# Queries of a second self attention by seven block products instead of eight, with the sums spread over the step order

## The chip, the cores and the metric

The kernel runs on one core of a Trainium2 chip. The metric is the device time of one launch in microseconds. The kernel is called several times; the median of the runs counts.

## The reference

A two-layer decoder over `x` of shape (8, 112, 512) in float32, six residual steps: layer 0 self attention, cross attention and a ternary feed forward, then layer 1 self attention, cross attention and a mixture feed forward. The change is in the layer 1 self attention (and, in name only, in the same function for layer 0). Cut to what matters (b = 8, s = 112):

```python
B, S, D = x.shape          # D = 512, H = 16 heads of DH = 128, 4 key heads
q = (x @ Wq.T).reshape(b, s, 16, 128)
k = (x @ Wk.T).reshape(b, s, 4, 128)
v = (x @ Wv.T).reshape(b, s, 4, 128)
q = q * cos + rotate_half(q) * sin          # the same for k
k, v = repeat(k, 4), repeat(v, 4)           # four query heads share a key head
scores = einsum('bhqd,bhkd->bhqk', q, k) * 128 ** -0.5
attn = softmax(scores)                      # the window masks nothing at s = 112
out = einsum('bhqk,bhkd->bhqd', attn, v).reshape(b, s, 2048)
return out @ Wo.T
```

## The kernel before

The 8 x 112 tokens are kept transposed in two halves `xT[hf]` of four batches (448 columns, four chunks of 128 features). `self_attention` (L526 on) runs eight turns (g, hf): four groups g of four query heads, each for both token halves. `pipeline` writes out TensorE's order by hand: while the scores and contexts of turn n are done, `weave` puts the steps of `prepare(n + 1)` and the output projections between them as filler, by a cost given with each step. The order on VectorE, ScalarE, GpSimd and SyncE is made by the scheduler of the tile framework, from the program's order and its own estimates.

One turn's preparation is one key tile `pr_k` and four query tiles `pr_q`. In `roped` (L605) a tile is four accumulating matmuls over 448 columns into one bank (`mm`, two buffers). ScalarE copies the bank to `raw` (L614), two DMAs of SyncE's queue write the rotated halves to `turned`, GpSimd multiplies `raw` with the cosines (L623), VectorE `turned` with the sines (L624), and GpSimd adds both (L625).

A turn has two units of two batches. `scores` (L677) fills a two-bank tile (`s`, two buffers). `softmax` takes the maximum on VectorE (L450), eight exponentials with sums on ScalarE (L453), the reciprocal on VectorE (L456), and multiplies on GpSimd (L460). TensorE transposes (L471), VectorE copies (L472), and `contexts` multiplies with the values (L695) into two `mm` banks that ScalarE copies to `oT` (L700).

The output projection of two neighbouring token tiles is already done by seven products: `out_pair` (L714 on) forms sums of blocks of `oT` (`os`, `block_sums`, L249 to L252) and differences of blocks of `Wo` (`wos`, one `lay(g)` of four instructions, L257 to L260, as one step at the end of a turn), and `sevens` (L262 on) runs the products 1, 6, 2 and 5, 7, 3, 4 over 256 columns. A set holds two banks at a time: 1 and 2 share bank x, 6 stands alone in y, then 5 and 3 share a new y, 7 and 4 a new z. After each product `put` reads the bank (ScalarE L747 for the first, VectorE L744 for the rest), and the next product in the same bank waits for that read. The tiles that make no pair go through `project_out` (L426, L430, read at L431).

Of the kernel before, what the change touches and what calls it, by code (L numbers as in the profile page):

```python
# [9 lines left out]
F32 = mybir.dt.float32  # L10
# [5 lines left out]
P = 128  # L16
# [141 lines left out]
def decoder(ctx: ExitStack, tc: tile.TileContext, i: dict, out: bass.AP):  # L158
# [84 lines left out]
        for k, (lhsT, rhs) in enumerate(pairs):  # L243
            nc.tensor.matmul(ps, lhsT, rhs, start=(k == 0), stop=(k == len(pairs) - 1))  # L244

    def block_sums(engines, s, a11, a12, a21, a22):

        e1, e2 = engines
        e1.tensor_tensor(s[0], a21, a22, ALU.add)  # L249
        e2.tensor_tensor(s[2], a11, a21, ALU.subtract)  # L250
        e1.tensor_tensor(s[1], s[0], a11, ALU.subtract)
        e1.tensor_tensor(s[3], a12, s[1], ALU.subtract)  # L252

    def block_differences(engines, t, b11, b12, b21, b22):

        e1, e2 = engines
        e1.tensor_tensor(t[0], b12, b11, ALU.subtract)  # L257
        e2.tensor_tensor(t[2], b22, b12, ALU.subtract)
        e1.tensor_tensor(t[1], b22, t[0], ALU.subtract)
        e1.tensor_tensor(t[3], b21, t[1], ALU.subtract)  # L260

    def sevens(products, put, width, name):  # L262


        bank = {}

        def product(n, at):
            pairs = products(n)
            for k, (lhsT, rhs) in enumerate(pairs):
                nc.tensor.matmul(  # L270
                    bank[at], lhsT, rhs, start=(k == 0 and n in (1, 6, 5, 7)), stop=(k == len(pairs) - 1),
                    skip_group_check=True,
                )
            put(n, bank[at])

        def first():
            for at in "yx":
                bank[at] = mm(f"p{at}_{name}")[:, :width]
            product(1, "x")
            product(6, "y")  # L280
            product(2, "x")

        def second():
            for at in "yz":
                bank[at] = mm(f"p{at}2_{name}")[:, :width]
            product(5, "y")
            product(7, "z")
            product(3, "y")
            product(4, "z")

        return first, second
# [234 lines left out]
    def self_attention(layer, following=None, behind=None, xT=None):  # L526
# [4 lines left out]
        half = width // 2  # L531
        turns = [(g, hf) for g in range(G) for hf in range(2)]
        held, matrices = [{} for _ in turns], {}
        dq, wos = [], {}

        if l0:
            pool, mid, top, tpool = (
# [50 lines left out]
        def extra(n):  # L588
            if n < 1:

                first, last = (0, 3 if l0 else 2) if n < 0 else (6, 8)
                steps = [(3.4, lambda b=b: values(b)) for b in range(first, last)]
                return steps + ([] if l0 or n < 0 else [(0.0, lambda: lay(0))])
            if not l0:
                return [] if n % 2 or n == len(turns) - 2 else [(0.0, lambda: lay(n // 2))]
            if n == 6:
                return [(0.6, rope) for _, rope in joined[0]["ropes"][4:]]
            steps = [(0.0, lambda k=k: add_bias(k)) for k in range(NT)] if n == 1 else []
            if n < 5:
                steps += [(0.0, lambda k=k: ternary_sum(tpool, k)) for k in range(4 * n - 4, 4 * n)]  # L600
            elif n == 5:
                steps += [(0.1, ternary_mean), (0.0, begin)]
            return steps

        def roped(dst, w, at, xh, bias, which, name):  # L605

            cos, sin = (
                const(f"{n}{which}{layer}").unsqueeze(1).to_broadcast([P, HB, T]) for n in ("cos", "sin")
            )
            ps = mm(f"pr_{name}")  # L610
            accumulate(ps[:, :HT], [(w[:, c, at : at + P], xh[:, c, :]) for c in range(NC)])
            raw = top.tile([P, HT], F32, tag="raw", bufs=3, name=f"raw_{name}")
            if bias is None:
                nc.scalar.copy(raw, ps[:, :HT])  # L614
            else:
                nc.scalar.activation(raw, ps[:, :HT], AF.Identity, bias=bias)

            turned = top.tile([P, HT], F32, tag="turned", bufs=3, name=f"turned_{name}")
            for at in range(0, P, half):
                other = at ^ half  # L620
                issued.append(nc.sync.dma_start(out=turned[at : at + half, :], in_=raw[other : other + half, :]).ins)
            by_batch = lambda t: t.rearrange("p (b t) -> p b t", b=HB)
            nc.gpsimd.tensor_tensor(by_batch(dst), by_batch(raw), cos, ALU.mult)  # L623
            nc.vector.tensor_tensor(by_batch(turned), by_batch(turned), sin, ALU.mult)  # L624
            nc.gpsimd.tensor_tensor(dst, dst, turned, ALU.add)  # L625

        def prepare(n):
            g, hf = turns[n]
# [17 lines left out]
                if not l0:  # L646
                    steps += entering(npool, xT, "at1", [6], 3)
            steps += [(3.0, lambda: roped(kT, wk, g * P, xT[hf], col("bk", g) if l0 else None, "k", f"k_{nm}"))]
            for c in range(4):
                steps.append((3.0, lambda c=c: roped(  # L650
                    qT[:, c, :], wq, c * P, xT[hf], col("bq", 4 * g + c) if l0 else None, "q",
                    f"q_{nm}_{c}",
                )))
            if n == 1:
                steps += [(3.4, lambda b=b: values(b)) for b in (4, 5)]
            if l0 and n == 0:
# [28 lines left out]
        def contexts(n, u):  # L685
            g, hf = turns[n]
            nm = f"{layer}_{g}_{hf}_{u}"
            kept = {}

            def add():  # L690

                po = [wide(f"po_{nm}_0")[:, 0, :]] if l0 else [mm(f"po_{nm}_{k}") for k in range(2)]
                for k, (b, s) in enumerate(parts(n, u)):
                    at, kv = slice(s * width, (s + 1) * width), g * (P // width) + s
                    nc.tensor.matmul(  # L695
                        po[0 if l0 else k][at, :HT], v[:, b, kv * width : (kv + 1) * width],
                        kept["pT"][:, 4 * k : 4 * k + 4, :].rearrange("p h q -> p (h q)"), start=True, stop=True,
                    )
                for k, b in enumerate(sorted({b for b, _ in parts(n, u)})):
                    nc.scalar.copy(oT[:, :, rows_of(b)], po[k][:, :HT].rearrange("p (h q) -> p h q", h=4))  # L700

            return probs_transposed(late, lambda: held[n]["p", u], kept, nm) + [(0.8 if l0 else 1.5, add, True)]

        def lay(g):

            b = matrices[g][1].rearrange("p (h k) (s n) -> p h k s n", h=2, s=2)
            t = dq[0].tile([P, 4, 2, D // 2], F32, tag="wos", bufs=1, name=f"wos_{layer}_{g}")
            wos[g] = t
            block_differences(
                (nc.vector, nc.gpsimd), [t[:, n] for n in range(4)],  # L710
                b[:, 0, :, 0], b[:, 0, :, 1], b[:, 1, :, 0], b[:, 1, :, 1],
            )

        def out_pair(g, k, nm):  # L714
# [5 lines left out]
                return slice((k + m) * P, (k + m + 1) * P)  # L720

            def add_up():
                s.append(dq[0].tile([P, 4, 2, P], F32, tag="os", bufs=1, name=f"os_{nm}"))
                block_sums(
                    (nc.vector, nc.gpsimd), [s[0][:, n] for n in range(4)],
                    a[:, 0, :, tok(0)], a[:, 1, :, tok(0)], a[:, 0, :, tok(1)], a[:, 1, :, tok(1)],
                )

            def products(n):
                b = matrices[g][1].rearrange("p (h k) (s n) -> p h k s n", h=2, s=2)  # L730
                t, v = wos[g], s[0]
                pick = {
                    1: lambda c: (a[:, 0, c, tok(0)], b[:, 0, c, 0]), 2: lambda c: (a[:, 1, c, tok(0)], b[:, 1, c, 0]),
                    3: lambda c: (v[:, 3, c], b[:, 1, c, 1]), 4: lambda c: (a[:, 1, c, tok(1)], t[:, 3, c]),
                    5: lambda c: (v[:, 0, c], t[:, 0, c]), 6: lambda c: (v[:, 1, c], t[:, 1, c]),
                    7: lambda c: (v[:, 2, c], t[:, 2, c]),
                }
                return [pick[n](c) for c in range(2)]

            def put(n, ps):  # L740
                if n == 1:
                    d.append(dq[0].tile([P, 2, 2, D // 2], F32, tag="od", bufs=1, name=f"od_{nm}"))
                d1, d2, d3 = d[0][:, 0, 1], d[0][:, 1, 0], d[0][:, 1, 1]
                add = lambda to, of: nc.vector.tensor_tensor(to, of, ps, ALU.add)  # L744
                x0, x1 = x[:, k, : D // 2], x[:, k, D // 2 :]
                if n == 1:
                    nc.scalar.copy(d1, ps)  # L747
                elif n == 6:
                    add(d2, d1)
                elif n == 2:  # L750
# [8 lines left out]
                else:  # L759
                    add(d2, d2)  # L760
                    nc.gpsimd.tensor_tensor(
                        x[:, k + 1, :], x[:, k + 1, :], d[0][:, 1].rearrange("p a b -> p (a b)"), ALU.add
                    )

            first, second = sevens(products, put, D // 2, nm)
# [29 lines left out]
        def go():  # L795
# [3 lines left out]
                joined.append(following(npool, late))  # L799
            if not l0:  # L800
                dq.append(stage_pool("dq"))
            oT = (pool if l0 else late).tile([P, 4, NB * T], F32, tag="oT", bufs=1, name=f"oT{layer}")
            pipeline(
                turns, HB if l0 else HB // 2, 2 if l0 else 1, prepare, scores, contexts, outputs, extra,
# [1086 lines left out]
```

## Time and profile before

| what | value |
|---|---|
| median of three runs (lowest, highest) | 1826.2 us (1821.77, 1830.13) |
| profiled execution, its span | 1825.17 us, 1823.4 us |
| granted TensorE clock, mean | 0.997 |
| busy: TensorE, VectorE, GpSimd, ScalarE | 1770.0, 942.3, 757.4, 652.6 us |
| second self attention, from its first scores to the end of its pair projections | about 927 to 1184 us |
| query matmuls in it (L244 pr_q, 256 records) | 101.5 us |
| set products over 256 columns in it (L270) | four records, 0.86 us in the chain |

Lines are those of the kernel before, in the change's version they are further down (`roped` L629 on, `paired` L664 on, rope L718 to L721, the maximum L466, transposes L487, the reads of the output sets L854 and L857). A float32 matmul leaves two records in the profile. PE is TensorE, PEld its weight loads, DVE VectorE, ACT ScalarE, POOL GpSimd, SP SyncE. "A <- B" in a list of waits means that A sat idle until B was done.

### The profile page before, as it was taken

What the parts mean: (1) busy time and instruction counts of PE and PEld (TensorE: products, weight loads), DVE (VectorE), ACT (ScalarE), POOL (GpSimd) and SP (SyncE); (2) the same over time, 40 slices, a digit from 0 to 9 for tenths busy, and PEclk for the clock granted to TensorE, in tenths of its full rate; (3) what the DMA queues carried; (4) which work ended last, traced back from release to release, by engine and by line L of the source; (5) the groups of instructions that cost most, each with busy time, mean ns of one, the idle gap of its engine ahead of it and who ended that gap; (6) DMA issues with size and microseconds to landing.
All of it is one profiled execution on the core that took longest, in us unless ns stands there. A gap on an engine that the chain in (4) does not pass through costs nothing.

```text
span 1823.4 us, 20355 instructions
## 1 busy us (share of the span) xinstructions
PE 1770.0 (97%) x7150; PEld 990.4 (54%) x7150; DVE 942.3 (52%) x1652; ACT 652.6 (36%) x1955; POOL 757.4 (42%) x664
## 2 busy tenths in 40 slices
PE   8999999999999999999999999999999999999998
PEld 4454544555455555567655665645654444554444
DVE  4455656645454544787433544435755444334444
ACT  2444443554333434465332232236733111031110
POOL 3454555355555640000134555512353354434533
PEclk9999999999999999999999999999999999999999
DMA  6132423143233112011121221210011212011101
GB/s 241 26 118 66 142 81 93 53 150 116 55 89 99 47 53 92 24 70 69 57 65 34 74 72 42 69 58 1 8 36 50 77 56 81 24 50 55 62 34 40
DMA packets 40429, 124.50 MB, mean 68 GB/s; under 512 B 7332, under 2 KB 20700, under 8 KB 32904
## 3 DMA queue, kind: packets, MB, share of 16 engines
q1 hardware_dynamic: 33192, 93.73, 16.1%
q0 software_dynamic: 6848, 29.36, 5.3%
q8 instruction: 56, 0.92, 0.2%
q14 instruction: 45, 0.37, 0.1%
q10 hardware_dynamic: 288, 0.12, 0.0%
HBM read 94.56 MB, written 10.28 MB: 57 GB/s over the span
## 4 chain that ended last, share of the span: by engine, by line
PE 81%; DVE 8%; ACT 3%; POOL 3%; DMA 2%; issue 1%; SPq 1%; ACTq 0%; POOLq 0%; DVEq 0%
PE pr_q L244 10%; PE pf L244 5%; PE po_x L980 4%; PE pb_dn L1526 4%; PE po_at L426 3%; PE pv L244 3%; PE po_at L430 3%; PE ps L677 3%; PE pr_k L244 3%; PE po L695 3%; PE pq_x L244 3%; PE po_x L426 2%; PE po_x L430 2%; PE pa_dn L1526 2%; PE ps_x L944 2%; PE pb_up L1526 2%
## 5 line engine op out<-in xcount | busy, mean ns | idle before, releaser
L244 PE MATMUL pr_q<-xT_at,wq 128*128 128x448 f32 x512 | 204.1, 543 | 0.0
L460 POOL TENSOR_TENSOR p<-p,total 112x896 f32<-112x896 f32 (+1 forms) x56 | 85.3, 1529 | 140.3 <-DVE total L456 133.2
L244 PEld LDWEIGHTS pr_q<-xT_at,wq 128*128 128x128 f32 x512 | 93.7, 190 | 84.5 <-issue 78.6
L453 ACT ACTIVATE p<-p,nmax 112x113 f32<-112x113 f32 x256 | 95.8, 376 | 109.7 <-DVE nmax L450 108.8
L1709 POOL TENSOR_TENSOR h<-silu,h 128x448 f32<-128x448 f32 x64 | 74.6, 1169 | 116.1 <-ACT silu L1707 115.9
L244 PE MATMUL pf<-h,sw 128*128 128x448 f32 x256 | 105.7, 539 | 0.0
L1103 POOL TENSOR_SCALAR tl<-tr,ternary_bounds 128x512 f32<-128x512 f32 x32 | 51.4, 1605 | 122.5 <-DMA tr<-in_c_w_dram 122.5
L1711 DVE TENSOR_TENSOR h<-h,share 128x448 f32<-128x448 f32 x48 | 41.3, 867 | 111.9 <-POOL h L1709 111.9
L950 DVE TENSOR_REDUCE nmax_x<-ps_x 112x2 f32<-112x750 f32 x64 | 57.1, 933 | 79.3 <-PE ps_x L944 79.3
L625 POOL TENSOR_TENSOR qT<-qT,turned_q 128x448 f32<-128x448 f32 x64 | 75.6, 1184 | 53.5 <-DVE turned_q L624 45.9
L980 PE MATMUL po_x<-pT_x,kv 125*128 125x448 f32 x192 | 89.3, 549 | 1.7 <-DVE pT_x L975 1.3
L623 POOL TENSOR_TENSOR qT<-raw_q,tables 128x448 f32<-128x448 f32 x64 | 77.6, 1218 | 23.5 <-ACT raw_q L614 16.0
L472 DVE COPY pT<-ppt 112x448 f32<-112x448 f32 x96 | 57.1, 617 | 58.1 <-PE ppt L471 58.1
L952 ACT ACTIVATE p_x<-ps_x,nmax_x 112x375 f32<-112x375 f32 x124 | 69.7, 574 | 38.2 <-DVE nmax_x L950 38.1
L1707 ACT ACTIVATE silu<-pf,cols 128x448 f32<-128x448 f32 x64 | 40.5, 633 | 118.7 <-PE pf L244 117.0
L1526 PE MATMUL pb_dn<-h,sums_dn 128*128 128x448 f32 x192 | 80.3, 541 | 1.0 <-DVE xT_ff L1748 0.5
L624 DVE TENSOR_TENSOR turned_q<-turned_q,tables 128x448 f32<-128x448 f32 x64 | 50.5, 789 | 47.2 <-DMA turned_q<-raw_q 46.7
L244 PEld LDWEIGHTS pf<-h,sw 128*128 128x128 f32 x256 | 48.7, 190 | 47.5 <-issue 41.0
L426 PE MATMUL po_at<-wo,oT 128*128 128x512 f32 x152 | 74.3, 611 | 0.0
L430 PE MATMUL po_at<-wo,oT 128*128 128x512 f32 x152 | 71.4, 592 | 0.0
L677 PEld LDWEIGHTS ps<-kT,qT 64*112 64x112 f32 (+1 forms) x768 | 58.0, 181 | 16.9 <-issue 10.0
L460 POOL TENSOR_TENSOR p_e<-p_e,total_e 112x896 f32<-112x896 f32 x16 | 26.9, 1682 | 96.9 <-DVE total_e L456 72.7
(358 smaller groups left out, 3920.7 us busy)
## 6 DMA issues: line engine op xcount, KB each, us to landing
tw<-in_c_w_dram SPq DMA_DIRECT2D x16, 512.0 KB
tr<-in_c_w_dram POOLq DMA_DIRECT2D x32, 256.0 KB, 4.0
signs<-tl POOLq DMA_DIRECT2D x32, 256.0 KB, 2.9
fup<-in_f_up_dram SPq DMA_DIRECT2D x8, 1024.0 KB
fdn<-in_f_dn_dram SPq DMA_DIRECT2D x8, 1024.0 KB
turned_q<-raw_q SPq DMA_DIRECT2D x128, 56.0 KB
turned_q<-raw_q SPq DMA_DIRECT2D x64, 112.0 KB
share<-gated SPq DMA_DIRECT2D x12, 448.0 KB
```

The lines of the kernel that those rows point to most:

```text
L244: nc.tensor.matmul(ps, lhsT, rhs, start=(k == 0), stop=(k == len(pairs) - 1))
L426: nc.tensor.matmul(ps[0], lhsT, rhs, start=(c == 0), stop=False)
L430: nc.tensor.matmul(ps[0], lhsT, rhs, start=False, stop=(c == len(pairs) - 1))
L453: nc.scalar.activation(p[:, h, :], src[:, h, :], AF.Exp, bias=nmax[:, h : h + 1], accum_out=total[:, h : h + 1])
L460: spread[:] = [nc.gpsimd.tensor_tensor(p[:, at, :T], p[:, at, :T], total[:, at], ALU.mult).ins]
L623: nc.gpsimd.tensor_tensor(by_batch(dst), by_batch(raw), cos, ALU.mult)
L625: nc.gpsimd.tensor_tensor(dst, dst, turned, ALU.add)
L677: nc.tensor.matmul(ps[:T, 4 * k + h, :T], qT[at, h, bcols(b)], kT[at, bcols(b)], start=True, stop=True)
L952: e = nc.scalar.activation(p[:, 2 * j + s, :], ps[:T, s, :L], AF.Exp, bias=nmax[:, s : s + 1], accum_out=total[:, 2 * j + s : 2 * j + s + 1],)
L980: nc.tensor.matmul(po[0][:, : 4 * T], kv[:, b, c, :], pTs[c], start=(c == 0), stop=(c == NLC - 1))
L1526: nc.tensor.matmul(bank[n], lhsT, rhs, start=(k == 0 and n in (1, 6, 7)), stop=(k == len(pairs) - 1), skip_group_check=True,)
L1709: nc.gpsimd.tensor_tensor(to, s, at["h1"][:, c, half(hf)], ALU.mult)
```

## The change

In layer 1 the query tiles of all turns but the first are made in pairs, by sets of seven products over 224 columns (half of a token half). The blocks of `Wq` are summed (`sums`, once per group, one result in place of a block of `Wq`), the blocks of `xT` are subtracted (`xs`, once per turn). All reads of the sets are on VectorE, so is the copy of `raw` where there is no bias and the first read of `out_pair`; the last rope addition of the second tile of the second pair moves from GpSimd to VectorE. The block sums are no longer one step: `block_sums` and `block_differences` return four steps, which are spread over the filler (`lay(g - 1)` between the query steps of a turn with hf = 0, `differ(n + 2)` and `add_up(g + 1)` at the end of a turn). They write some results in place, GpSimd does one of the differences and the last sum of `os` where VectorE did. The contexts of layer 1 use a score tile (`s`) instead of two `mm` banks. `sevens` takes its first bank in the other order, except in the second set of a turn.

```diff
-    def block_sums(engines, s, a11, a12, a21, a22):
+    def block_sums(engines, new, s, a11, a12, a21, a22):
...
-        e1.tensor_tensor(s[0], a21, a22, ALU.add)
-        e2.tensor_tensor(s[2], a11, a21, ALU.subtract)
-        e1.tensor_tensor(s[1], s[0], a11, ALU.subtract)
-        e1.tensor_tensor(s[3], a12, s[1], ALU.subtract)
...
+        return [
+            one, lambda: e2.tensor_tensor(a21, a11, a21, ALU.subtract),
+            lambda: e1.tensor_tensor(s(1), s(0), a11, ALU.subtract),
+            lambda: e2.tensor_tensor(s(2), a12, s(1), ALU.subtract),
+        ]
...
         def first():
-            for at in "yx":
+            for at in "yx" if turned else "xy":
                 bank[at] = mm(f"p{at}_{name}")[:, :width]
...
-            for at in "yz":
+            for at in "yz" if turned else "zy":
...
             if not l0:
-                return [] if n % 2 or n == len(turns) - 2 else [(0.0, lambda: lay(n // 2))]
+                g, hf = turns[n]
+                after = differ(n + 2) if n + 2 < len(turns) else []
+                if hf == 0 and g + 1 < G:
+                    after += add_up(g + 1)
+                after = later(after)
+                return after
...
+            if bias is None:
+                nc.vector.tensor_copy(raw, ps[:, :HT])
...
+        def paired(turn, qT, c, nm):
...
+            def products(n):
+                a = matrices[g][0].rearrange("p (h k) (c m n) -> p h k c m n", h=2, c=2, m=2)
+                b = xT[hf].rearrange("p (h k) (s t) -> p h k s t", h=2, s=2)
+                s, t = sums[g], xs[turn]
+                pick = {
+                    1: lambda k: (a[:, 0, k, c, 0], b[:, 0, k, 0]), 2: lambda k: (a[:, 1, k, c, 0], b[:, 1, k, 0]),
+                    3: lambda k: (s[:, 2, k, c], b[:, 1, k, 1]), 4: lambda k: (a[:, 1, k, c, 1], t[:, 3, k]),
+                    5: lambda k: (s[:, 0, k, c], t[:, 0, k]), 6: lambda k: (s[:, 1, k, c], t[:, 1, k]),
+                    7: lambda k: (a[:, 0, k, c, 1], t[:, 2, k]),
+                }
+                return [pick[n](k) for k in range(2)]
+
+            def put(n, ps):
+                if n == 1:
+                    raw[:] = [new_raw(f"q_{nm}_{2 * c + m}") for m in range(2)]
+                r0, r1 = raw
+                add = lambda to, of: nc.vector.tensor_tensor(to, of, ps, ALU.add)
+                if n == 1:
+                    nc.vector.tensor_copy(r0[:, tok[1]], ps)
+                elif n == 6:
+                    add(r1[:, tok[0]], r0[:, tok[1]])
...
+                elif n == 3:
+                    add(r0[:, tok[1]], r1[:, tok[0]])
+                    rotated(qT[:, 2 * c, :], r0, "q", f"q_{nm}_{2 * c}")
+                else:
+                    add(r1[:, tok[0]], r1[:, tok[0]])
+                    rotated(qT[:, 2 * c + 1, :], r1, "q", f"q_{nm}_{2 * c + 1}", nc.vector if c else nc.gpsimd)
+
+            first, second = sevens(products, put, half_, f"q_{nm}_{c}", c == 1)
+            return [(2.3, first), (3.0, second)]
...
+                if n == 1:
+                    steps[-1:-1] = later(differ(1))
+                more = [step for c in range(2) for step in paired(n, qT, c, nm)]
+                if hf == 0:
+                    more = [step for pair in zip(more, later(lay(g - 1))) for step in pair]
+                steps += more
...
-                po = [wide(f"po_{nm}_0")[:, 0, :]] if l0 else [mm(f"po_{nm}_{k}") for k in range(2)]
+                pair = wide(f"po_{nm}")
+                po = [pair[:, k, :] for k in range(2)]
...
                 if n == 1:
-                    nc.scalar.copy(d1, ps)
+                    nc.vector.tensor_copy(d1, ps)
```

## The prediction

> **What bounds the kernel now.** First the page's busy line, for the engine that has no room:
>
> ```profile
> PE 1770.0 (97%) x7150; PEld 990.4 (54%) x7150; DVE 942.3 (52%) x1652; ACT 652.6 (36%) x1955; POOL 757.4 (42%) x664
> ```
>
> TensorE is the bound on average. Whether it is in the edited stage is read from busy time by stretch, one line for each of two neighbouring turns of the second self attention (930 to 1200 us); the columns are PE, PEld, DVE, ACT and POOL busy, clock, DMA.
>
> ```profile
> 982.60:1018.00 35.40, 35.40 (x155) 23.84 (x154) 15.99 (x30) 10.91 (x43) 20.73 (x18) 1.00 0.31 93
> 1018.00:1052.80 34.80, 32.82 (x135) 20.19 (x134) 17.79 (x27) 10.53 (x42) 19.45 (x17) 1.00 0.16 33
> ```
>
> The first turn has TensorE busy in every microsecond at full clock, the second idles 2.0 us. VectorE has half of a turn free, GpSimd 40%. Third, the chain of waits, in order of time, inside the second turn, for lengths and for that idle time:
>
> ```profile
> 1034.99 0.75 PE pr_q L244 x2
> 1035.75 0.86 PE px_at_True L270 x4
> 1036.61 0.93 PE py_at_True L270 x4
> ...
> 1042.32 1.73 DVE wos L257
> 1044.04 0.02 issue
> 1044.07 1.64 DVE wos L259
> 1045.71 1.01 DVE nmax L450
> ...
> 1049.77 0.56 DVE x L431
> 1050.34 0.04 issue
> 1050.38 1.02 PE po L695 x2
> ```
>
> A product of a set over 256 columns takes 0.86 us (four records; each matmul leaves two). Two large differences (wos, 512 elements) hold VectorE, the read of `po_at` comes late, and the second context matmul waits for that bank. TensorE's waits in the stage have only one such row:
>
> ```profile
> PE po L695 <- DVE x L431: 4.0, 2, 2.0
> ```
>
> Last, the timelines of GpSimd and VectorE side by side, because the change gives both more work (start, length):
>
> ```profile
> 1025.86 1.13 POOL L623 TENSOR_TENSOR qT<-raw_q,tables 128x448 f32<-128x448 f32 x1
> 1027.61 1.14 POOL L625 TENSOR_TENSOR kT<-kT,turned_k 128x448 f32<-128x448 f32 x1 [0.62 <-DVE turned_k L624]
> ```
>
> ```profile
> 1026.17 1.30 DVE L624 TENSOR_TENSOR turned_k<-turned_k,tables 128x448 f32<-128x448 f32 x1 [0.89 <-DMA turned_k<-raw_k]
> 1027.82 1.41 DVE L624 TENSOR_TENSOR turned_q<-turned_q,tables 128x448 f32<-128x448 f32 x1 [0.34 <-DMA turned_q<-raw_q]
> ```
>
> The VectorE multiply takes 0.62 us elsewhere. Both times here it ends about half a microsecond after GpSimd's instruction does: over the 0.82 us that the first overlaps GpSimd it loses 0.68. Two instructions that read only SBUF take turns. VectorE's adds that read a PSUM bank do not: L744 is 0.41 to 0.42 us in every row, also beside GpSimd.
>
> **TensorE's part.** A pair of query tiles is two runs of pr_q (3.01 us each in the chain), 6.02 us. It becomes seven products over 224 columns: 0.86 x 224/256 = 0.753 us each, 5.27 us. Saved 0.75 us a pair; 7 turns (the first keeps the plain form) x 2 pairs = **10.5 us**. Bounds for a product: 0.753, and 0.863 as at 256 columns, which would leave nothing. I take 0.753: scores with only 112 columns run 16 records in 1.57 us, 0.098 us each, near proportion, while their weight loads last 0.18 to 0.19 us, so loads do not limit short matmuls.
>
> **Contexts in score tiles.** The two waits of 2.0 us end with the bank that caused them. Next late is the second scores matmul: scores, context, scores now alternate over two tiles, so it needs the exponentials of the first to be read. In the shown turn these end at 1049.6, and TensorE could be there at 1049.3. Gain 2 x (2.0 - 0.3) = **3.4 us**; bounds 0 and 4.0.
>
> **VectorE reads.** Copies of raw tiles leave ScalarE (0.53 us each, beside TensorE's work, worth nothing). VectorE gets, for each set, seven reads of 224 columns at 0.39 us (0.42 at 256, less 32 columns; bounds 0.36 and 0.42), 5.4 us a turn. A read starts 0.20 us after its product ends, so it is over 0.16 us before the next product is: alone it costs nothing, but that slack is all there is, since `sevens` has two banks and every product after the second waits for a read. The copies of `od` (0.4 us) and one rope addition in four (0.62) come too; `os` loses one VectorE instruction and gains one on GpSimd.
>
> **The sums, and the queue they stand in.** Each turn needs three `xs` instructions of 448 elements on VectorE and one on GpSimd; each group two `sums` instructions of 512 on each. The built order puts them right behind the last query set, between the reads of the following output set. I play one such turn through; zero is the end of the last query product, O1, O6, O2, O5, O7, O3, O4 are the output products of 0.86 us, GpSimd's instructions are 1.13 us.
> GpSimd multiplies raw 2 from -0.1 to 1.03, so xs 1 ends at 1.6, the read of O1 at 2.0, and O2 (which reuses that bank) starts at 2.05 instead of 1.72. GpSimd's own xs runs to 2.73, xs 2 to 3.25, the read of O6 to 3.65: O5 at 3.7, 0.79 late again. GpSimd multiplies raw 3 to 4.4, xs 3 ends at 4.9, the read of O2 at 5.3: O7 at 5.35, 0.79. The turned multiply and O5's read end at 6.3: O3 0.14. GpSimd's add runs to 7.1, the second turned multiply to 7.6, O7's read to 8.0: O4 0.84 late. Together 2.9 us, in the preparations of turns 2, 4 and 6.
> In turns 3 and 5 `sums` 1 stands before the read of the last query product and `sums` 2 and the rope addition before O7's read, and GpSimd has its 1.27 us sum in between. The same play gives delays of 0.9, 0.8, 2.6 and 1.2 us, 5.5 each. In turn 1 two value products (6.9 us) stand there; eight such VectorE instructions and six of GpSimd, taking turns, end about 11 us after the last but one read, and the scores, due at 7.8, wait 3.3. Turn 7 has no sums: 0.5. Inside the query sets the turned multiplies stand between reads: 0.2 a turn, 1.4. Sum 3 x 2.9 + 2 x 5.5 + 3.3 + 0.5 + 1.4 = **24.9 us** of new waits. Bounds: if VectorE never met GpSimd, the same order with 0.62 and 0.68 us gives 0.65 (turns 2, 4, 6), 2.2 (3, 5), 0.3, 0.4 and 0.7 in all sets: 7.8 us. If GpSimd wins every tie, some 8 us more than 24.9.
>
> The Trainium skill speaks against this change: SBUF — State Buffer, section "SBUF: two separate sides", says that VectorE instructions with two SBUF inputs and GpSimd share a port pair as an exclusive lock, the loser fully blocked. The rows above show 0.14 us of progress in 0.82; by the rule it would be none, about 0.1 us more for each of some five blocked instructions a turn, an estimate of 3.5 us on top.
>
> Moved at no cost: the rotating DMAs stay as many on SP's queue, in the same order; they now leave in twos at the end of a set, about 2.95 us from raw to turned as in the trace, and their arrival (2.8 in the play) is earlier than VectorE gets to them. If that cover went, each late microsecond would reach the scores after the output set.
>
> **Sum.** -10.5 - 3.4 + 24.9 = +11.0 us. The profiled execution took 1825.17 us (span 1823.4 and 1.8 around it); 1836.2. The median of the runs is 1.0 above it: **1837 us**.
>
> **Rivals.** *The sums fit* (faster): VectorE finds GpSimd idle or waiting, waits stay near 7.8 us, and -10.5 - 3.4 + 7.8 = -6.1 gives 1820; with all hidden 1812. It decides below 2.0 us of new wait a turn (13.9/7). For it: VectorE is half idle. Against: GpSimd is busy 20 of 35 us before, gets some 2.4 us a turn more, and its instructions sit exactly behind the same set. *Short products do not pay*: 224 columns cost as much as 256; the 10.5 us are gone, and with the waits of the first rival it is 1831. Against it the 112-column scores. *The score tile is the new wait*: with three large differences ahead of the maximum, the second scores wait up to 1.7 us more in four turns, 7 us on the first rival's time, 1827. That the change does not do what it says is excluded by the built order: seven products of two matmuls stand where eight double-width matmuls stood.
>
> **How the numbers follow.** Within 0.5%, about what a measurement of this kernel can tell from no change, is 1817 to 1835. Main case 0.58: it lies around 1837 and reaches to 1845, of this 0.45 above 1835 and 0.13 below. The sums fit 0.27: 0.13 below 1817, 0.14 within. Short products 0.08: 0.06 within, 0.02 slower. Score tile 0.07, within. Faster 0.13, within 0.40, slower 0.47. The range 1816 to 1845 leaves out the best hiding and the worst ties; the main case alone is 1828 to 1845.
>
> **What would show it.** Right: query products of 0.75 us in the chain; no wait of po for L447; TensorE waiting for VectorE's output reads (L854, L857) 2 to 6 us a turn, and xs instructions of 1.1 us instead of 0.62. Wrong: turns without TensorE waits (then 1812 to 1820), or products of 0.86 us.

## The result, and the profile after

| | median, us (lowest, highest) | ratio to before (95% interval) |
|---|---|---|
| before | 1826.33 (1821.56, 1834.95), 20 runs | |
| after | 1833.57 (1828.86, 1839.01), 20 runs | 1.0036 (1.0024 to 1.0049) |

The change makes the kernel slower by 0.36%, 6.6 us (4.4 to 8.9). The forecast was 1837, its sum +11.0 us. The profiled execution of after took 1839.01 us with a span of 1837.2 us, at a mean granted clock of 0.992 instead of 0.997. It lies 5.4 us above the median, at a lower clock, so the comparisons below are made inside the stage, in stretches at full clock where nothing else is said. 0.36% is inside the 0.5% that the prediction counts as the same; its likeliest case had 0.13 of its 0.58 there.

First the busy line of after's page. TensorE has 168 more records and 5.7 us more busy time; VectorE gained 77 us:

```profile
PE 1775.7 (97%) x7318; PEld 1022.3 (56%) x7318; DVE 1019.4 (55%) x1798; ACT 628.2 (34%) x1906; POOL 779.1 (42%) x681
```

Busy time by stretch of after, for the turns of hf = 0 and hf = 1 in the middle of the stage (columns as before: length, then PE, PEld, DVE, ACT, POOL busy, clock, DMA):

```profile
1062.48:1099.16 36.68, 35.29 (x178) 27.81 (x177) 25.80 (x52) 7.53 (x36) 22.53 (x20) 1.00 0.30 90
1099.16:1135.30 36.14, 32.53 (x158) 24.20 (x157) 28.14 (x47) 7.53 (x36) 24.09 (x19) 1.00 0.15 32
```

Before, these were 35.40 and 34.80. TensorE's busy time did not rise in the second (32.53 against 32.82), but its idle time went from 2.0 to 3.6 us, and in the first from none to 1.4. The list of TensorE's waits in the stage says for whom (us in total, times, longest):

```profile
PE ps L781 <- POOL qT L721: 5.8, 2, 3.3
PE pz_at_True L286 <- DVE x L854: 5.4, 5, 2.0
PE pz_at_True L286 <- DVE od_at_True L854: 3.0, 5, 0.8
PE py_at_True L286 <- DVE od_at_True L854: 1.7, 5, 0.3
PE pz_q L286 <- DVE raw_q L688: 0.9, 1, 0.9
```

The waits of the contexts for L447 are gone. In their place stand the output set's banks, which wait for VectorE's reads. The chain of waits shows the query products inside a set at 0.76 us, and a pair of context matmuls at 1.50 instead of 1.69:

```profile
1068.39 0.77 PE py_q L286 x4
1069.16 0.76 PE pz_q L286 x4
1069.92 0.76 PE py_q L286 x4
...
1074.23 1.50 PE po L800 x4
```

Then one output set, in turn 4: the timelines of VectorE, GpSimd and TensorE (start, length).

```profile
1079.42 1.02 DVE L267 TENSOR_TENSOR xs<-xT_at 128x448 f32<-128x448 f32 x1
1080.36 0.41 DVE L857 COPY od_at_True<-px_at_True 128x256 f32<-128x256 f32 x1
1080.69 1.22 DVE L271 TENSOR_TENSOR xs<-xT_at,xs 128x448 f32<-128x448 f32 x1
1081.83 0.41 DVE L854 TENSOR_TENSOR od_at_True<-od_at_True,py_at_True 128x256 f32<-128x256 f32 x1
1082.16 1.22 DVE L272 TENSOR_TENSOR xs<-xT_at,xs 128x448 f32<-128x448 f32 x1
1083.30 0.41 DVE L854 TENSOR_TENSOR x<-x,px_at_True 128x256 f32<-128x256 f32 x1
```

```profile
1078.82 1.14 POOL L719 TENSOR_TENSOR qT<-raw_q,tables 128x448 f32<-128x448 f32 x1 [0.61 <-DVE raw_q L688]
1079.91 1.51 POOL L270 TENSOR_TENSOR xs<-xT_at 128x448 f32<-128x448 f32 x1
1081.39 1.51 POOL L719 TENSOR_TENSOR qT<-raw_q,tables 128x448 f32<-128x448 f32 x1
```

```profile
1082.29 1.13 PE L286 MATMUL py_at_True<-wos,os_at_True 128*128 128x256 f32 x4 [0.34 <-DVE od_at_True L854]
1083.86 1.10 PE L286 MATMUL pz_at_True<-wo,oT 128*128 128x256 f32 x4 [0.43 <-DVE x L854]
1086.38 1.13 PE L286 MATMUL pz_at_True<-wos,oT 128*128 128x256 f32 x4 [0.55 <-DVE od_at_True L854]
```

Each read (0.41 us in every row) stands behind an xs instruction that lasts 1.0 to 1.2 instead of 0.62 us, and each product behind a read. The first two lists also show how the two engines meet. The three xs instructions end at 1080.44, 1081.91 and 1083.38, each 0.48 or 0.49 us after the GpSimd instruction beside them (1079.96, 1081.42, 1082.90); and GpSimd's two of 1.51 us end 0.98 and 0.99 us after an xs instruction. Alone they last 0.62 and 1.13 us. So each engine stands until the other's instruction is through: they take turns, and do not share.

From its first product to the scores the set takes 8.43 us; seven products of 0.86 are 6.03, and in the trace of before every set took 6.11. In this trace the three sets with xs take 8.43 to 8.44, turn 5's, with xs and sums, 10.69 (turn 3's, in a turn with a mean clock of 0.95, 11.28), turn 7's, with neither, 6.85.

### The profile page after: what moved, and what is told of

Its sections match the earlier page's. It is cut to its first block, busy times and chain, and to the rows that moved or that the text cites. A ratio compares the mean times of both kernels' runs of the same rounds, so it can differ in the third digit from the quotient of the medians.

```text
span 1837.2 us, 20839 instructions
## 1 busy us (share of the span) xinstructions
PE 1775.7 (97%) x7318; PEld 1022.3 (56%) x7318; DVE 1019.4 (55%) x1798; ACT 628.2 (34%) x1906; POOL 779.1 (42%) x681
## 4 chain that ended last, share of the span: by engine, by line
PE 80%; DVE 9%; POOL 3%; ACT 3%; issue 3%; DMA 1%; SPq 0%; ACTq 0%; DVEq 0%; POOLq 0%
PE pr_q L244 6%; PE pf L244 5%; PE po_at L442 4%; PE po_x L1092 4%; PE po_at L446 3%; PE pb_dn L1638 3%; PE ps L781 3%; PE po L800 3%; PE pr_k L244 3%; PE pv L244 3%; PE pq_x L244 3%; PE po_x L442 2%; PE po_x L446 2%; PE pa_dn L1638 2%; PE ps_x L1056 2%
## 5 line engine op out<-in xcount | busy, mean ns | idle before, releaser
L244 PE MATMUL pr_q<-xT_at,wq 128*128 128x448 f32 x288 | 115.2, 545 | 0.0
L721 POOL TENSOR_TENSOR qT<-qT,turned_q 128x448 f32<-128x448 f32 x57 | 68.3, 1200 | 46.5 <-DVE turned_q L720 34.0
L469 ACT ACTIVATE p<-ps,nmax 112x112 f32<-112x112 f32 x128 | 43.3, 368 | 123.2 <-DVE nmax L466 123.2
L244 PEld LDWEIGHTS pr_q<-xT_at,wq 128*128 128x128 f32 x288 | 52.4, 190 | 47.9 <-issue 44.8
L781 PE MATMUL ps<-kT,qT 64*112 64x112 f32 (+1 forms) x768 | 62.8, 270 | 5.8 <-POOL qT L721 5.8
```

What stands on the lines that cost most here:

```text
L469: nc.scalar.activation(p[:, h, :], src[:, h, :], AF.Exp, bias=nmax[:, h : h + 1], accum_out=total[:, h : h + 1])
L721: last.tensor_tensor(dst, dst, turned, ALU.add)
L781: nc.tensor.matmul(ps[:T, 4 * k + h, :T], qT[at, h, bcols(b)], kT[at, bcols(b)], start=True, stop=True)
```

## The experiments

All ratios are to the kernel before, on the same chip; "set" is the time from the first output product to the scores, as above. Differences "by the medians" go across chips, on which the kernel before took 1825.0 to 1826.3 us.

**e1: the contexts alone.** On the kernel before, one line:

```diff
-                po = [wide(f"po_{nm}_0")[:, 0, :]] if l0 else [mm(f"po_{nm}_{k}") for k in range(2)]
+                pair = wide(f"po_{nm}")
+                po = [pair[:, k, :] for k in range(2)]
```

> The kernel before with one part of the change alone: the contexts of the second self attention go into a score tile instead of two mm banks. Theory (the trace of after: the two po waits of 2.0 us are gone and a pair of context matmuls lasts 1.50 instead of 1.69 us, some 15 pairs): -4.0 - 0.19 x 15 = -6.9 us, ratio 0.996. The prediction's step: -3.4 us (ratio 0.998), no shorter context matmuls. Rival 'score tile is the new wait': the second scores wait up to 1.7 us in four turns, so 0 to +3 us.

1817.04 us, ratio 0.9952 (0.9936 to 0.9968). The two kinds of turn, by stretch:

```profile
1048.11:1083.31 35.20, 35.20 (x154) 24.01 (x153) 17.29 (x33) 10.73 (x43) 21.69 (x20) 1.00 0.30 93
1083.31:1116.35 33.04, 32.59 (x133) 20.25 (x133) 18.23 (x26) 10.35 (x42) 18.80 (x16) 1.00 0.17 35
```

The turn with the wait got 1.73 us shorter, close to the prediction's 1.7 (2.0 less 0.3), though not in its parts: the new wait for the exponentials is 0.45, and shorter context matmuls give 0.2 back. The other turns gain those 0.2, turn 1 0.5 and the end of the stage 1.0. At equal clock the stage is 5.6 us shorter, more than the 3.4 forecast; the runs say 8.0 by the medians (5.8 to 11.7 by the interval). So the change's best part lies in these lines, and the rest of it costs more than the whole change shows. The rival in which the second scores wait is out: they wait 0.9 us in all, in two places.

**e2: the xs differences once per token half.**

```diff
-                after = differ(n + 2) if n + 2 < len(turns) else []
+                after = differ(n + 2) if n == 0 else []
...
-                xs[n] = dq[0].tile([P, 4, 2, HT // 2], F32, tag="xs", bufs=1, name=f"xs_{layer}_{n}")
+                xs[n] = dq[0].tile([P, 4, 2, HT // 2], F32, tag="xs", bufs=2, name=f"xs_{layer}_{n}")
+                for later_n in range(n + 2, len(turns), 2):
+                    xs[later_n] = xs[n]
```

> After with one part less: the xs differences depend on the token half alone, so they are made for turns 1 and 2 and used again by the turns of the same half (3, 5, 7 and 4, 6); their four instructions behind the last query set are gone in four places. To make room the weights of the next sub-layer are loaded later and turned has two buffers instead of three in this stage. Theory (the queue of VectorE behind the last query set is what TensorE waits for): the output sets of turns 4 and 6 fall from 8.44 to about 6.7 us, those of turns 3 and 5 by some 3 us each (only sums left): -1.8 x 2 - 3 x 2 = -9.6 us against after, so about 1824, ratio 0.998 to 0.999. Rival (the waits have another cause, the rotating multiplies and the raw reads): under 3 us gained, ratio 1.002 to 1.004.

1822.16 us, ratio 0.9979 (0.9969 to 0.9989): 11.4 us below after by the medians.

```profile
1050.38:1085.47 35.09, 34.51 (x178) 28.00 (x177) 23.10 (x49) 7.53 (x36) 20.82 (x20) 1.00 0.32 94
1085.47:1118.80 33.33, 32.43 (x158) 24.13 (x157) 25.33 (x44) 7.53 (x36) 22.60 (x18) 1.00 0.16 35
```

The sets are 6.85 and, where sums are left, 7.65 us: twenty instructions behind the last query set were worth 1.6 and 3.0 us a turn. Yet the two turns together are no shorter than e1's, where the queries are plain: 68.42 against 68.24 us.

**e3: GpSimd quiet beside the output set.** VectorE's instructions and their order stay.

```diff
-            nc.gpsimd.tensor_tensor(by_batch(dst), by_batch(raw), cos, ALU.mult)
+            if not quiet:
+                nc.gpsimd.tensor_tensor(by_batch(dst), by_batch(raw), cos, ALU.mult)
...
-            return block_differences(
+            one, _, two, four = block_differences(
...
+            return [one, two, four]
```

> After with GpSimd made quiet beside the output sets, VectorE's instructions and their order kept. Left out: the multiplication by the cosines of the second pair of query tiles of each turn (its rope addition takes raw instead) and GpSimd's xs difference (product 7 reads another xs block). Theory 'shared SBUF access' (an xs instruction of VectorE lasts 1.2 instead of 0.62 us because GpSimd runs beside it): xs instructions on VectorE fall to 0.62 to 0.8 us, the output set of turns 2, 4, 6 from 8.44 to 6.4 to 6.9 us, of turn 5 from 10.7 to 8 to 9.5 (its sums and the rope addition still meet GpSimd): -2 x 3 - 2 x 2 = -10 us against after, ratio 0.997 to 0.999. Rival 'queue alone' (the instructions are long in themselves or in that order): xs rows stay at 1.2, sets at 8.4 and 10.7, ratio 1.003 to 1.004.

1820.44 us, ratio 0.9979 (0.9967 to 0.9991). VectorE's timeline in turn 4:

```profile
1067.55 0.62 DVE L267 TENSOR_TENSOR xs<-xT_at 128x448 f32<-128x448 f32 x1
1068.10 0.42 DVE L859 COPY od_at_True<-px_at_True 128x256 f32<-128x256 f32 x1
1068.44 0.61 DVE L271 TENSOR_TENSOR xs<-xT_at,xs 128x448 f32<-128x448 f32 x1
1068.98 0.42 DVE L856 TENSOR_TENSOR od_at_True<-od_at_True,py_at_True 128x256 f32<-128x256 f32 x1
1069.32 0.62 DVE L272 TENSOR_TENSOR xs<-xT_at,xs 128x448 f32<-128x448 f32 x1
```

The same three instructions, in the same order, now last 0.62 us, and the sets 6.8 to 7.0 us (8.7 with sums, where the first xs instruction still meets GpSimd and lasts 1.61). In the sets without sums the first five steps from product to product are 0.86 us, as if no xs stood there; what is left of the loss is the step to product 4, behind the second turned multiplication and the rope addition. So it is not the number of instructions in the queue: at 0.62 each the xs instructions fit. It is that VectorE and GpSimd both work on SBUF at that moment. This is the cause the prediction put down. The time, too, is what "the sums fit" forecast (1820), with this part of GpSimd's work left out.

**e4: two copies back on ScalarE.**

```diff
-                nc.vector.tensor_copy(raw, ps[:, :HT])
+                nc.scalar.copy(raw, ps[:, :HT])
...
-                    nc.vector.tensor_copy(d1, ps)
+                    nc.scalar.copy(d1, ps)
```

> After with two copies given back to ScalarE: the copy of raw of the tiles that are no pair (eight keys and turn 0's queries) and the first read of each output set. Theory (first scores of the stage waited 3.30 us instead of 2.30 because turn 0's raw copies stand in VectorE's queue): -1.0 us there, and 0.2 us in each of five output sets with sums: -2 us against after, ratio about 1.0025. Rival (ScalarE is late itself, 0.53 us a copy, behind exponentials): the first read comes later, 0 to +3 us against after, ratio 1.0036 to 1.005.

1847.03 us, ratio 1.0115 (1.0098 to 1.0133). A miss, even beyond its rival. Two things went wrong, the first in turn 4's first query set (TensorE, then ScalarE), the second on VectorE:

```profile
1070.03 1.02 PE L286 MATMUL py_q<-xs,sums 128*128 128x224 f32 x4 [1.08 <-ACT raw_k L635]
```

```profile
1069.41 0.57 ACT L635 COPY raw_k<-pr_k 128x448 f32<-128x448 f32 x1
```

```profile
1084.28 1.43 DVE L271 TENSOR_TENSOR xs<-xT_at,xs 128x448 f32<-128x448 f32 x1
1085.74 1.43 DVE L272 TENSOR_TENSOR xs<-xT_at,xs 128x448 f32<-128x448 f32 x1
```

The copy of the key tile stands behind eight exponentials, and product 6 reuses its bank: the step from product 1 to 6 grows from 0.88 us to between 1.6 and 2.0 in six turns. With the first output read gone from VectorE's queue the scheduler puts all xs instructions in one run, and product 5 waits for the read behind them (2 to 3 us). The first scores still wait 3.3 us, so the copies of turn 0 are not what delays them. What the run points to is who owns the small loss in the first query set of turns 2 to 7 in after (0.88 and 0.86 instead of 0.76 us for the first two steps): the bank of the key tile. In turn 1, where a transpose stands between the key tile and product 1, these steps are 0.77 and 0.76.

**e5: the sums behind the output reads.** The same instructions as after, in another place.

```diff
-                after = later(after)
-                return after
+                def behind_read(f):
+                    with tc.issue_after(read[-1].ins):
+                        f()
+                return [(0.0, lambda f=f: behind_read(f)) for f in after]
...
-                    add(d2, d2)
+                    read.append(add(d2, d2))
```

> After with the same instructions in another place: from turn 1 on the xs differences and the sums are not free to stand behind the last query set, each is issued behind the last read of the output set that was written out before it (L854 of product 4). Nothing is left out and nothing is stored twice. Theory (the place is the price): the output sets of turns 2, 4, 6 fall from 8.44 to 6.85 us and those of turns 3 and 5 from 10.7 to about 7, with 0 to 1 us a turn given back where sums stand ahead of a maximum: -1.6 x 3 - 3.7 x 2 + 1 = -11 us against after, about 1822, ratio 0.998. Rival (the amount of VectorE and GpSimd work is the price, wherever it stands): the waits move to the scores and transposes of the same turns and the time stays at 1832 to 1835, ratio 1.003 to 1.005.

1826.95 us, ratio 1.0002 (0.9989 to 1.0014): 6.6 us below after, some 60% of what was expected. All sets fall to 6.85 to 6.92. But in turns 3 and 5 the sums, xs and wos now stand together, beside GpSimd, and the key tile's copy behind them is late (VectorE, then TensorE in the next preparation):

```profile
1055.47 1.64 DVE L272 TENSOR_TENSOR wos<-wo,wos 128x512 f32<-128x512 f32 x1
1057.03 1.90 DVE L253 TENSOR_TENSOR os_at_True<-oT 128x256 f32<-128x256 f32 x1
...
1060.31 0.61 DVE L638 COPY raw_k<-pr_k 128x448 f32<-128x448 f32 x1
```

```profile
1060.98 1.02 PE L286 MATMUL py_q<-xs,sums 128*128 128x224 f32 x4 [1.48 <-DVE raw_k L638]
```

The two preparations behind them take 37.56 and 37.55 us, against 36.68 in after. Both theories hold in part. The place is a price, and where two kinds of sums meet the amount is one too.

**e6: turn 1's sums later, and the first pair's additions in the other order.** On e5:

```diff
-                return steps + ([] if l0 or n < 0 else later(differ(2) + add_up(1)))
+                return steps + ([] if l0 or n < 0 else [
+                    (0.0, lambda f=f: behind_read(f)) for f in differ(2) + add_up(1)
+                ])
...
-                    rotated(qT[:, 2 * c, :], r0, "q", f"q_{nm}_{2 * c}")
+                    late_add = rotated(qT[:, 2 * c, :], r0, "q", f"q_{nm}_{2 * c}", None if c == 0 else nc.gpsimd)
...
+                    if c == 0:
+                        with tc.issue_after(added.ins):
+                            nc.gpsimd.tensor_tensor(qT[:, 0, :], qT[:, 0, :], raw[2], ALU.add)
```

> The kernel of the run before with two more moves of instructions, none added: turn 1's xs and sums are issued behind its last rope addition, and in the first pair of a turn GpSimd adds the second tile first, so that VectorE's second multiplication with the sines no longer runs beside a GpSimd addition (1.53 us beside it, 0.62 alone). Theory: the query sets' steps from product 7 to 3 and 3 to 4 fall from 0.96 and 0.86 to 0.76 us, -0.3 x 7 = -2.1 us; turn 1's wait for qT falls from 2.5 to under 1 us, -1.5 us; in all -3.6 us against the run before, about 1818, ratio 0.996; the turns with both kinds of filler then come to 34.8 and 32.4 us against 35.2 and 33.0 without query sets. Rival (the steps are late because a multiplication of 0.62 us stands between two reads at all): 0.05 to 0.1 us a step gained, under 1 us; turn 1's sums come late for the maximum or for turn 2's products instead: no gain.

1821.36 us, ratio 0.9966 (0.9953 to 0.9978), 5.6 us below e5 where 3.6 was expected. VectorE's second multiplication with the sines is 0.62 instead of 1.53 us (the row is from turn 5), and the steps from product 7 to 3 and 3 to 4 are 0.76 instead of 0.96 and 0.86, in every turn.

```profile
1099.88 0.62 DVE L731 TENSOR_TENSOR turned_q<-turned_q,tables 128x448 f32<-128x448 f32 x1
```

So the loss inside the second query set had the same cause as the output sets': a VectorE instruction of two SBUF inputs beside a GpSimd one. Turn 1's wait for `qT` is gone (only the stage's first one of 3.3 us is left). The turns expected at 34.8 and 32.4 us came in part: turn 2 takes 34.91 and turns 3 and 5 32.83 and 32.12, but turns 4 and 6 37.25 and 37.05, because the late copy of the key tile stays as in e5.

**e7: all of it, and GpSimd alone for the additions.** On after: xs once (e2), late sums (e5, e6), group 0's sums behind turn 0's last rope addition, and both pairs' additions on GpSimd, second tile first:

```diff
-                    rotated(qT[:, 2 * c + 1, :], r1, "q", f"q_{nm}_{2 * c + 1}", nc.vector if c else nc.gpsimd)
+                    added = rotated(qT[:, 2 * c + 1, :], r1, "q", f"q_{nm}_{2 * c + 1}", nc.gpsimd)
+                    with tc.issue_after(added.ins):
+                        nc.gpsimd.tensor_tensor(qT[:, 2 * c, :], qT[:, 2 * c, :], raw[2], ALU.add)
```

> All that the runs before point to, together, on after: xs made once per token half (two tiles), sums issued behind the output reads, turn 1's behind its last multiplication, the sums of group 0 issued behind the last rope addition of turn 0, and in both pairs of a turn GpSimd adds the second tile first and then the first one (VectorE keeps the multiplications alone). Theory (the products save 0.75 us a pair as soon as nothing on VectorE stands between the reads): output sets of 6.05 to 6.1 us in all turns, query sets' steps 7 to 3 and 3 to 4 of 0.76 us, first scores back to a wait of 2.3 us, turns of some 34.0 and 31.7 us instead of 35.2 and 33.0 without query sets: about 1810, ratio 0.991, 7 us below the kernel with the contexts alone. Rival (the pairs cannot pay, another wait comes up in the scores, since GpSimd's two additions end late): ps waits 0.5 to 1 us a turn and the time is 1815 to 1818, ratio 0.994 to 0.996.

1821.60 us, ratio 0.9975 (0.9964 to 0.9985): the rival's outcome, and slower than that. The sets do come down to 6.04 to 6.05 us from turn 3 on. The wait moved to the set behind them, 8.25 instead of 7.0 us. GpSimd, VectorE and TensorE there:

```profile
1074.68 1.32 POOL L714 TENSOR_TENSOR qT<-qT,turned_q 128x448 f32<-128x448 f32 x1
...
1078.21 1.26 POOL L889 TENSOR_TENSOR x<-x,od_at_True 128x512 f32<-128x512 f32 x1
```

```profile
1079.50 0.42 DVE L875 COPY od_at_False<-px_at_False 128x256 f32<-128x256 f32 x1 [1.28 <-POOL x L889]
```

```profile
1079.98 1.13 PE L286 MATMUL px_at_False<-wo,oT 128*128 128x256 f32 x4 [1.14 <-DVE od_at_False L875]
```

GpSimd's later additions push its addition into x, which reads the one buffer of `od`; the next set's first read waits for that buffer. What the rival named is there too: the scores wait for GpSimd's last additions in four places, 2.7 us in all, 1.8 of them in one.

**e8: the change without its contexts.** After with the line of e1 undone.

> After with the contexts of the second self attention back in two mm banks. Theory (the score tile is worth the same here as alone): 7 us slower than after, about 1840, ratio 1.0075. Rival (the differences of Wo, spread over the query steps, have already removed the late bank read, so that the score tile saves only the shorter context matmuls): +2 to +4 us, ratio 1.005. Second rival (contexts between the products take the banks that the next set needs): more than +10 us, ratio over 1.009.

1843.90 us, ratio 1.0102 (1.0082 to 1.0122): 10.3 us slower than after by the medians, 6.8 in turns 1 to 7 of the two traces (294.1 against 287.3 us). By the runs that is the price of the second rival (over 10 us, ratio over 1.009), by the traces that of the theory. What the second rival describes is there: the contexts now stand between products and share their banks. They wait for reads of query products in six places, 2.9 us in all, and for L447 in two, 1.9 us.

```profile
1073.58 1.85 PE L799 MATMUL po<-pT,v 112*128 112x448 f32 x4 [0.48 <-DVE raw_q L694]
```

So the score tile is worth at least as much here as alone, and without it the change would have been 1% slower. Why runs and traces differ by 3.5 us stays open.

**e9 and e10: what the query sets are worth at their best.** e9 is e7 with the second pair's additions as in the change:

```diff
...
-                    added = rotated(qT[:, 2 * c + 1, :], r1, "q", f"q_{nm}_{2 * c + 1}", nc.gpsimd)
+                    added = rotated(qT[:, 2 * c + 1, :], r1, "q", f"q_{nm}_{2 * c + 1}", nc.vector if c else nc.gpsimd)
...
```

> The kernel of e7 with the second pair's additions as in the change (GpSimd the first tile, VectorE the second); the first pair keeps GpSimd for both, second tile first. Theory (e7 lost its gain because GpSimd's two late additions hold up its x addition, which reads od_at_True, so that the next set's first read waits for that tile): the next set falls back from 8.25 to 7.0 us, the first output set rises from 6.05 to 6.85; turns with a pair set 34.8 us, others about 32.7, against 35.2 and 33.0 with the contexts alone: 1813 to 1816, ratio 0.993 to 0.995. Rival (the pairs cannot win anything, one wait takes another's place): 1817 to 1821, ratio 0.995 to 0.998.

> The contexts alone once more, on the same chip as e9, so that the two can be compared: 1817 us, ratio 0.995. If the query sets are worth anything e9 is 1 to 4 us below it; if not, at it or above.

e9: 1821.33 us, ratio 0.9972 (0.9961 to 0.9982). e10, e1's kernel again: 1816.37 us, ratio 0.9957 (0.9944 to 0.9970). The two kinds of turn, e9 first:

```profile
1052.02:1086.95 34.93, 34.39 (x178) 27.97 (x177) 22.58 (x49) 7.52 (x36) 21.28 (x20) 1.00 0.31 94
1086.95:1120.26 33.31, 31.98 (x158) 24.16 (x157) 25.05 (x44) 7.41 (x36) 20.93 (x18) 1.00 0.16 35
```

```profile
1047.24:1082.43 35.19, 35.19 (x153) 24.00 (x153) 17.30 (x33) 10.73 (x43) 21.69 (x20) 1.00 0.31 93
1082.43:1115.47 33.04, 32.59 (x134) 20.25 (x133) 18.22 (x26) 10.35 (x42) 18.81 (x16) 1.00 0.17 35
```

68.24 us for two turns with query sets, 68.23 without. TensorE is busy 1.4 us less in them and idle 1.4 us more; the four pairs' 3.0 us went there and into steps between products. The next set did fall back to 7.0 and the first to 6.85 as expected, group 0's move brought the first scores' wait from 3.3 to 2.2 us, and the expected 32.7 of the second turn became 33.3: there a sum and a difference of 1.76 and 1.75 us stand ahead of a maximum on VectorE, and the matmuls behind it wait 0.8 us. The medians of e9 and e10 are 5.0 us apart, which these turns do not show; the run of each with a mean clock of 0.999 took 1816.71 and 1815.96 us. The lowest median of all is that of the one-line change of e1.

## Why the prediction was right, and which terms were off

The forecast case is what happened: the products save what they should, and VectorE's reads behind xs and sums, slowed by GpSimd, take more. The point, 1837, is 3.4 us above the median. The outcome with the highest chance, over 0.5% slower (0.47), did not come; the median lies in the band that had 0.40. Term by term, at full clock:

| term of the sum | predicted | measured |
|---|---|---|
| 14 pairs of query tiles | -10.5 | -10.5 (0.76 a product in the chain) |
| contexts in score tiles | -3.4 | -5.6 alone (e1), -6.8 within the change (e8) |
| output sets of turns 2, 4, 6 | 2.9 each | 2.4 each (8.43 less 6.03) |
| output sets of turns 3, 5 | 5.5 each | 4.7 in turn 5 |
| turn 1's scores | 3.3 | 2.5 |
| turn 7 | 0.5 | 0.8 |
| inside query sets | 1.4 in all | 5.3, and one wait of 0.9 |
| first scores of the stage | 0 | 1.0 |

With -6.8 for the contexts the measured column gives +9.8 us. Between the traces the stage, from its first scores to the next sub-layer's first projection, grew by 8.2 us. One turn of each trace ran at a clock of 0.95 to 0.96: turn 5 before lost 1.5 us against turn 3, turn 3 after lost 0.8 beside the wait of 0.9 in the table. With these two taken out the growth is 9.0: 1.0 up to turn 1, 8.0 from there on. So under 1 us of the ledger is open (2 us with -5.6 for the contexts). The runs say 6.6, with an interval that reaches 8.9, a little under both figures.

That the point is so near is in part luck. Against the measured column the sum is off by 3.4 us at the contexts, by 3.6 at the output sets and the scores of turn 1, and by 5.8 the other way inside the query sets and at the first scores; what is left is 1.2.

**The cause was right.** e3 takes part of GpSimd's work away and leaves VectorE's order as it is; the sets fall to 6.8. The play of the order behind the last query product had the two engines take turns, as they do, and was a little harsh: it ended GpSimd's instruction 1.13 us after VectorE's and VectorE's 0.5 to 0.57 us after GpSimd's, where the trace has 0.99 and 0.48. That fits a set's loss of 2.4 instead of 2.9 us.

The prediction read its rows, 0.14 us of progress in 0.82 us of overlap, as milder than the rule, and by the rule it put an estimate of 3.5 us on top, 1840.5. The section "SBUF: two separate sides" of SBUF — State Buffer in the Trainium skill speaks of an exclusive lock whose loser is fully blocked. The trace of after agrees with it: of VectorE's instructions of 448 elements on SBUF alone that stand behind a GpSimd one in this stage, those of 0.85 us and those of 1.69 us end 0.48 us after it alike. The 0.14 us are thus the same however long the overlap is, and the play had them in; the 3.5 us on top were not called for. That 1837 lies nearer to the median than 1840.5 is no test of the rule, because other terms were off by as much.

**The step that was most mis-sized is "inside the query sets 0.2 a turn".** It was 0.76. The prediction counted the multiplications with the sines alone. Two more things stand there: the copy of the key tile, moved to VectorE, holds the bank of product 6 (0.88 and 0.86 us for the first two steps; e4 and e5 make this wait long enough to be named), and GpSimd's rope addition runs beside the second multiplication (e6 removes that part, 0.3 a turn). The rows of after for the second, in turn 4, on GpSimd, VectorE and TensorE:

```profile
1075.33 1.14 POOL L721 TENSOR_TENSOR qT<-qT,turned_q 128x448 f32<-128x448 f32 x1 [1.74 <-DMA turned_q<-raw_q]
```

```profile
1075.41 1.53 DVE L720 TENSOR_TENSOR turned_q<-turned_q,tables 128x448 f32<-128x448 f32 x1
```

```profile
1076.33 0.92 PE L286 MATMUL pz_q<-xs,wq 128*128 128x224 f32 x4
1077.29 1.02 PE L286 MATMUL py_q<-xT_at,sums 128*128 128x224 f32 x4
1078.15 0.92 PE L286 MATMUL pz_q<-xs,wq 128*128 128x224 f32 x4
```

The steps between these starts are 0.96 and 0.86 us. The last 0.2 a turn are steps of 0.77 to 0.82 us beside transposes and contexts; no run takes them apart.

**The contexts were mis-sized on the other side.** The two waits were worth what was said, 1.73 each. Not counted were 0.2 us in each later turn of hf = 0, 0.5 in turn 1 and 1.0 behind the last turn.

**Left out was the first scores' wait.** Group 0's sums put GpSimd's difference in `wq` (L256) ahead of the last rope addition. GpSimd's timeline of after:

```profile
930.90 1.52 POOL L256 TENSOR_TENSOR wq<-wq 128x512 f32<-128x512 f32 x1 [2.12 <-issue]
932.38 1.57 POOL L721 TENSOR_TENSOR qT<-qT,turned_q 128x448 f32<-128x448 f32 x1
```

The scores wait 3.3 us for that addition instead of 2.3. e9 issues the sums behind it, and the wait is 2.2.

**The rivals.** *The sums fit* fails on GpSimd, as e3 shows; its point of decision, 2.0 us of new wait a turn, was passed with some 3.9 (the measured waits of the table, 27.1 us, over seven turns). *Short products do not pay* is out by the 0.76 us in the chain. *The score tile is the new wait* is out by e1 and e8.

## What to carry to other kernels

A change that trades TensorE time for element-wise work is priced by where that work stands in its engine's queue and by what the other engine on SBUF does at that moment, not by the engine's idle share: VectorE had half of each turn free, and 1.6 to 3.0 us a turn were still lost in one place. Ask of each instruction that stands between two reads of a bank whether the other engine can hold it up: in the output sets one of 0.62 us cost nothing (e3, steps of 0.86 us), and the same one held up to 1.2 us cost 0.6 to 0.7 us a product. Take a change of several parts apart: here one line was worth more than the whole, and the part that gave the change its name was worth nothing in the trace even after five repairs (by the medians of e9 and e10 rather less, with intervals that overlap).

## What the runs showed that was not expected

- VectorE and GpSimd hold each other up in both directions, one whole instruction at a time. In after, xs instructions on VectorE last 1.22 us beside GpSimd and 0.62 without it (e3), and GpSimd's 1.13 us multiplication becomes 1.51. A small VectorE sum of 256 elements took 1.90 us in e5, where it takes 0.42 elsewhere: it ends 0.28 us after a GpSimd instruction of 2.13 us. VectorE's reads of a bank are not held up (0.41 us in the same rows).
- A matmul over 224 columns keeps its proportion to one over 256: 0.76 us for four records against 0.86, also with weight loads of 0.19 us between them.
- Taking an instruction off an engine's queue can make that queue worse: in e4 the read that had parted the xs instructions was gone, they came in one run, and the sets grew from 10.7 to 13.5 us.
